# Layer 0's softmax sums over keys: folded from 128 to 64 partitions and summed for two steps in one TensorE pass, a group later

## The chip, the core and the metric

The kernel runs on one core of a Trainium2 chip. The time is the device time of one execution in microseconds (us); lower is better. In the profile PE is TensorE (PEld its weight loads), DVE is VectorE, ACT is ScalarE, POOL is GpSimd, and SP is SyncE, whose queue issues most of the DMAs. A name like L443 is line 443 of the kernel before.

## The reference

Two cross attentions follow each other. Layer 0 takes x (2 x 2048 x 512) as queries and a context of 128 tokens per batch as keys and values, with 16 heads of 64 and a mask over the keys:

```python
attn = jnp.einsum('bqhd,bkhd->hbqk', qh, kh)
attn = attn * mask[None]
attn = attn - jnp.max(attn)
attn = jnp.exp(attn) * mask[None]
attn = attn / (jnp.sum(attn, axis=-1, keepdims=True) + 1e-15)
out = jnp.einsum('hbqk,bkhd->bqhd', attn, vh).reshape(Bn, Tq, H * DK)
out = out @ Wo + bo
x = out + residual          # and a layer norm with gamma and beta
```

Layer 1 is a plain softmax attention of 16 heads of 32 on the result, again with residual and layer norm. The change concerns one term of layer 0: `jnp.sum(attn, axis=-1)`, the sum over the 128 keys for each query and head. All is in 32-bit floats.

## The kernel before, in words

The queries are cut into NB = 8 blocks t of TB = 512 tokens, and layer 0's heads into NG = 4 groups g of four heads. A pair (t, g) is one step; the list `order` holds the 32 steps so that two steps of the same g and neighbouring blocks stand together. The loop at the end of layer 0 (its variable is i, from 0 to 15) takes two steps at a time; one turn of it is called a group below. The order of the instructions on every engine is the order in which the program is written, since the schedule is manual; tiles wait for each other through buffers that rotate in their pool (two `mm` and two `av` buffers in PSUM, four `p1` buffers of which each holds the probabilities of one step).

A turn of the loop with i > 0 does this:

- `queries_pair` makes the queries of the two steps with seven half-size products (L347, TensorE) in the order 1, 6, 7, 2, 5, 4, 3. Each product is two matmuls into one PSUM buffer. ScalarE copies product 1 (L368) and VectorE adds the others up (L359, L361). Between these, `exponentials0` is called for the two steps of the previous group, `before[0]` after product 1 and `before[1]` after product 2's addition: VectorE reduces the maxima of all partitions (L428, L429), ScalarE takes the exponentials (L432), and GpSimd multiplies with the mask (L433). So the reduction for `before[1]` stands in VectorE's queue ahead of the two additions that read product 5.
- `scores0` of the first step: TensorE multiplies keys and queries (L395, `st`), the keys on the 128 partitions of the result. VectorE applies the mask and takes each partition's maximum (L407). SyncE writes the maxima to DRAM (L416, `top`), waits for this to land, and reads them back onto all partitions (L419, `every`).
- `attend0` of the first step of the previous group: four matmuls with a matrix of ones (L443, `den`), one for each head and side by side in four column strips of 32, sum the probabilities over the keys; ScalarE copies the sums out (L445). Eight matmuls (L451, `psu`) multiply the probabilities with the values in two halves, and ScalarE copies each (L455). SyncE stores the sums (L456, 8 KB) and the result (L459, `u`, 512 KB).
- `scores0` and `attend0` again, for the second step of the group and the second of the group before.

SyncE's queue thus holds per group: `top`, `every`, `den`, `u`, and once more `top`, `every`, `den`, `u`. In some groups loads of x and masks (the masks on GpSimd's queue) come first, and `token_sums_1` and `token_sums_2` put eight additions on VectorE when g is 3. While p is 0 (i from 0 to 3) `keys0` comes ahead of the queries. In the last turn only the first `attend0` is called; the last three steps are attended to after the loop, and then layer 1 begins. Layer 1's own order is written out in `steps`. The rows g1 and b1, layer 1's gamma and beta, are loaded during layer 0's start and first used in layer 1.

Of the kernel before, what the change touches and what calls it, by code (L numbers as in the profile page):

```python
# [16 lines left out]
P = 128  # L17
# [7 lines left out]
def two_cross_attentions(  # L25
# [98 lines left out]
    def chunks(w):  # L124
        return w.rearrange("(c p) m -> p c m", p=P)
# [80 lines left out]
    with tc.tile_pool(name="w1", bufs=1) as w1, tc.tile_pool(name="a2", bufs=2) as a2, tc.tile_pool(  # L206
# [129 lines left out]
        def queries_pair(p, g, before):  # L336

            a, b = 2 * p, 2 * p + 1
            e0, e1 = 2 * g, 2 * g + 1
            (a11, a12), (a21, a22) = halves0(g)  # L340
            (b11, b21), (b12, b22) = xts[a], xts[b]
            t1, t2, t4 = zip(*(token_sums[p, c] for c in range(2)))

            def product(n, w, x, tile_of):
                ps = tile_of(f"ps{n}_{p}_{g}")
                for c in range(2):
                    nc.tensor.matmul(  # L347
                        ps, w[:, c, :], x[c] if isinstance(x, tuple) else x[:, c, :],
                        start=(c == 0), stop=(c == 1),
                    )  # L350
                return ps

            def q_tile(t, e):
                queries[t, e] = four.tile([P, TB], F32, tag="q", name=f"q0_{t}_{e}")
                return queries[t, e]

            def add(out, ps, sb, bias=None):
                if bias is None:
                    nc.vector.tensor_tensor(out, ps, sb, ALU.add)  # L359
                else:  # L360
                    nc.vector.scalar_tensor_tensor(  # L361
                        out=out, in0=ps, scalar=bias, in1=sb, op0=ALU.add, op1=ALU.add
                    )

            less1 = db0[:, e0 : e0 + 1]
            c11 = q_tile(a, e0)
            ps = product(1, a11, b11, mm_tile)
            nc.scalar.activation(c11, ps, AF.Identity, bias=bq0s[:, e1 : e1 + 1])  # L368
            exponentials0(*before[0])
            c12 = q_tile(b, e0)  # L370
            add(c12, product(6, s2[:, g], t2, mm_tile), c11)
            c21 = q_tile(a, e1)
            add(c21, product(7, a21, b12, av_tile), c12)
            add(c11, product(2, a12, b21, av_tile), c11, less1)
            exponentials0(*before[1])
            c22 = q_tile(b, e1)
            ps = product(5, s1[:, g], t1, mm_tile)
            add(c22, ps, c21)
            add(c12, ps, c12, less1)
            add(c21, product(4, a22, t4, mm_tile), c21)  # L380
            add(c12, product(3, s4[:, g], b22, av_tile), c12)

        tops0, probs0 = {}, {}
        last4 = w1.tile([P, 4], F32, tag="last4", name="last4")
        order = [(2 * p + n, g) for p in range(NB // 2) for g in range(NG) for n in range(2)]

        def scores0(t, g):

            b, _ = where(t)
            st = sc_tiles(f"st_{t}_{g}", [2, TB])  # L390
            for n in range(2):
                q = queries.pop((t, 2 * g + n))
                for j in range(2):
                    rows = slice(j * DK, (j + 1) * DK)
                    nc.tensor.matmul(  # L395
                        st[n][:, j, :], k0[rows, 2 * g + n, b * K : (b + 1) * K], q[rows, :],
                        start=True, stop=True,
                    )
            pair = fours.tile([P, 2, 2, TB], F32, tag="p1", name=f"sm_{t}_{g}")
            n0 = 2 * (order.index((t, g)) - len(order) + 2)  # L400
            if n0 >= 0:
                top = last4[:, n0 : n0 + 2]
            else:
                top = a2.tile([P, 2], F32, tag="top", name=f"top_{t}_{g}")
            for n in range(2):
                sm = pair[:, n]
                nc.vector.tensor_tensor_reduce(  # L407
                    out=sm, in0=st[n], in1=masks[t].unsqueeze(1).to_broadcast([P, 2, TB]),
                    scale=1.0, scalar=-3.4028234e38, op0=ALU.mult, op1=ALU.max,
                    accum_out=top[:, n : n + 1],  # L410
                )
                probs0[t, 2 * g + n] = sm
            if n0 >= 0:
                return

            nc.sync.dma_start(top_dram[t, g], top)  # L416
            every = a2.tile([P, 2 * P], F32, tag="every", name=f"every_{t}_{g}")
            flat = top_dram[t, g].rearrange("p n -> (p n)").unsqueeze(0)
            nc.sync.dma_start(every, flat.to_broadcast([P, 2 * P]))  # L419
            tops0[t, g] = every  # L420

        def exponentials0(t, g):
# [7 lines left out]
            for n in range(2):  # L430
# [3 lines left out]
                    s, s, masks[t].unsqueeze(1).to_broadcast([P, 2, TB]), ALU.mult  # L434
                )

        def attend0(t, g):

            b, _ = where(t)
            p = [probs0[t, 2 * g + j // 2][:, j % 2, :] for j in range(4)]  # L440
            ps = av_tile(f"den0_{t}_{g}")
            for j in range(4):
                nc.tensor.matmul(ps[32 * j : 32 * (j + 1), :], ones, p[j], start=True, stop=True)  # L443
            den = a4.tile([P, TB], F32, tag="den", name=f"dens0_{t}_{g}")
            nc.scalar.copy(den, ps)  # L445
            u = a3.tile([P, 2, TB], F32, tag="u", name=f"u0_{t}_{g}")
            for half in range(2):
                ps = av_tile(f"psu0_{t}_{g}_{half}")
                for j in range(4):
                    d = (4 * g + j) * DK + half * 32  # L450
                    nc.tensor.matmul(  # L451
                        ps[32 * j : 32 * (j + 1), :], v0[:, b, d : d + 32], p[j],
                        start=True, stop=True,
                    )
                nc.scalar.copy(u[:, half, :], ps)  # L455
            nc.sync.dma_start(  # L456
                den_rows(den_dram, t, g), den.rearrange("(j n) q -> j n q", n=32)[:, 0, :]
            )
            nc.sync.dma_start(u_dram[t, g], u.rearrange("p j q -> p (j q)"))  # L459

        bo0s, g0s = row(const, bo0, "bo0"), row(const, g0, "g0")
        g1s, b1s = row(const, g1, "g1"), row(const, b1, "b1")
        b0cs = columns(const, b0c, "b0c")
        g0cs = columns(const, g0c, "g0c")

# [10 lines left out]
        for i in range(len(order) // 2):  # L476
            p, g = i // NG, i % NG
            steps0 = order[2 * i : 2 * i + 2]
            if g == (2 if p == 0 else 1) and p + 1 < NB // 2:
                for t in (2 * p + 2, 2 * p + 3):  # L480
                    load_x(t)
                    masks[t] = load_mask(t)
            if p == 0:
                for e in (2 * g, 2 * g + 1):
                    keys0(e)
            if i == 1:
                for n in range(E // TB):
                    values0(1, n)
            if i == 4:
                w = w1.tile([P, 2 * ND, TB], F32, tag="first", name="wkv1")  # L490
                wk1s, wv1s = w[:, :ND, :], w[:, ND:, :]
                nc.sync.dma_start(wk1s, chunks(wk1))
                nc.sync.dma_start(wv1s, chunks(wv1))
            if i == 12:
                sums0(0, w1, "sums0", 1)
            if i == 13:
                load_wo0()

            if i == 0:
                queries0(0, 0)  # L500
                queries0(0, 1)
            else:
                queries_pair(p, g, order[2 * i - 2 : 2 * i])
            if i == len(order) // 2 - 1:
                for n in range(NG):
                    fetch_u(0, n)
            scores0(*steps0[0])
            if i == 0:
                queries0(1, 0)
                queries0(1, 1)  # L510
                weight_sums(1)
            else:
                attend0(*order[2 * i - 2])
            if i == 0:
                token_sums_1(0)
            elif g == NG - 1 and p + 1 < NB // 2:
                token_sums_1(p + 1)
            scores0(*steps0[1])
            if i == 0:
                for n in range(E // TB):  # L520
                    values0(0, n)
                token_sums_2(0)
                weight_sums(2)
            elif i < len(order) // 2 - 1:
                attend0(*order[2 * i - 1])
            if g == NG - 1 and p + 1 < NB // 2:
                token_sums_2(p + 1)
            if i in (1, 2):
                weight_sums((3, 0)[i - 1])
# [568 lines left out]
    for t in range(-1, NB):  # L1098
        go(steps(t))
        if t == -1:  # L1100
            nc.sync.dma_start(wo1s, chunks(wo1))
    t = NB - 1
    for i in range(NQ):
        project1(t, i, 0)
# [76 lines left out]
```

## Time and profile before

| what | value |
|---|---|
| median of 3 runs | 991.02 us (990.36 to 991.05) |
| the profiled execution | 989.38 us, of which the span of the core is 987.40 us |
| granted TensorE clock | 0.997 of full speed |
| TensorE busy, 45 to 398 us (layer 0's loop and its tail) | 353.0 of 353.0 us |
| VectorE, ScalarE, GpSimd busy in the same stretch | 184.5, 139.7, 158.5 us |
| one `den` matmul on record (L443), 256 records for 128 matmuls | 605 ns each, four at a time |
| ACT 128x2048 (L926); DVE 128x2048 (L858); POOL 128x1024 (L433) | 1912; 2278; 2368 ns |

A row of a timeline gives the start and duration in us, the engine, the line, the operation with its output and input, how many instructions were merged in the row, and in brackets how long the engine sat idle before it and what ended that. A matmul of 32-bit floats is on record twice, so "x8" are four matmuls. The chain of waits is followed back from the last instruction to what released each piece; a piece of it names what the end of the kernel depended on at that time.

### The profile page before, as it was taken

How to read it: one execution, taken by the hardware profiler on the slowest of the kernel's cores; microseconds unless marked ns; L12 is line 12 of the kernel's file. 1: busy time of each engine (PE TensorE's matmuls, PEld its weight loads, DVE VectorE, ACT ScalarE, POOL GpSimd, SP SyncE). 2: the span in 40 equal slices, each digit the busy share in tenths (PEclk: the TensorE clock that was granted, in tenths of full speed). 3: DMA queues.
4: the chain of work that ended last, by engine and by line, in shares of the span. 5: the costliest groups of instructions: out<-in, count | busy, mean ns of one | idle time of the engine just before them, and what ended most of it. 6: DMA issues, size and time to landing. Idle time of an engine off the chain costs nothing.

```text
span 987.4 us, 12723 instructions
## 1 busy us (share of the span) xinstructions
PE 968.7 (98%) x4628; PEld 451.3 (46%) x4628; DVE 658.9 (67%) x1060; ACT 382.4 (39%) x626; POOL 483.4 (49%) x403
## 2 busy tenths in 40 slices
PE   9999999999999999999999999999999999999996
PEld 5444333333333334474634644645545545445432
DVE  2544645565464553148569869869789689698866
ACT  1133434343443434134544434444344444344251
POOL 1043454443344455594454834925826736545143
PEclk9999999999999999999999999999999999999998
DMA  9324254124223443634643542632723724504311
GB/s 341 138 49 140 55 173 154 55 76 146 75 55 84 142 129 126 202 114 152 220 158 95 180 162 89 220 124 87 257 86 115 252 93 151 164 2 139 120 43 42
DMA packets 51325, 128.46 MB, mean 130 GB/s; under 512 B 9440, under 2 KB 13280, under 8 KB 47680
## 3 DMA queue, kind: packets, MB, share of 16 engines
q1 hardware_dynamic: 49536, 125.03, 38.4%
q0 software_dynamic: 1152, 2.10, 0.7%
q8 instruction: 36, 0.59, 0.3%
q10 hardware_dynamic: 576, 0.53, 0.2%
q14 instruction: 25, 0.20, 0.1%
HBM read 101.46 MB, written 26.18 MB: 129 GB/s over the span
## 4 chain that ended last, share of the span: by engine, by line
PE 88%; DVE 5%; DMA 3%; POOL 2%; issue 1%; ACT 1%; POOLq 0%; SPq 0%; DVEq 0%; ACTq 0%
PE pso L626 21%; PE ps L347 18%; PE pso L980 9%; PE psq L777 7%; PE st L395 6%; PE psu L451 5%; PE mx L828 3%; PE den L443 3%; PE s L902 3%; PE u L950 3%; DMA p<-rows 2%; PE psk L261 2%; PE psq L815 1%; PE psq L328 1%; PE psv L273 1%
## 5 line engine op out<-in xcount | busy, mean ns | idle before, releaser
L433 POOL TENSOR_TENSOR sm<-sm,mask 128x1024 f32<-128x1024 f32 x64 | 150.1, 2368 | 212.7 <-ACT sm L432 212.7
L626 PE MATMUL pso<-wo,uT 128*128 128x512 f32 x512 | 229.3, 599 | 0.5 <-POOL uT L182 0.5
L626 PEld LDWEIGHTS pso<-wo,uT 128*128 128x128 f32 x512 | 94.6, 190 | 117.5 <-issue 108.5
L613 POOL TENSOR_TENSOR rstd<-rstd,mhalf 128x1 f32<-128x1 f32 x64 | 35.2, 550 | 216.3 <-DVE shift L617 216.2
L980 PE MATMUL pso<-wq,ctx 128*128 128x512 f32 x256 | 115.4, 600 | 0.0
L407 DVE CUSTOM_DVE_ANT_1 sm<-st,mask 128x1024 f32<-128x1024 f32 x64 | 75.8, 1221 | 47.9 <-issue 23.5
L432 ACT ACTIVATE sm<-sm,ncs 128x1024 f32<-128x1024 f32 x64 | 69.9, 1140 | 70.1 <-DVE ncs L429 69.9
L844 ACT ACTIVATE e<-mx,less 128x128 f32<-128x128 f32 x224 | 61.0, 383 | 83.3 <-DVE less L841 83.3
L921 DVE TENSOR_TENSOR p<-s,p 128x1024 f32<-128x1024 f32 x56 | 65.9, 1219 | 40.2 <-PE s L902 28.1
L926 ACT ACTIVATE p<-p 128x2048 f32<-128x2048 f32 x28 | 53.5, 1912 | 97.0 <-DVE p L921 95.5
L359 DVE TENSOR_TENSOR q<-ps,q 128x512 f32<-128x512 f32 x75 | 51.6, 689 | 59.1 <-PE ps L347 31.8
L347 PE MATMUL ps<-xt,wq 128*128 128x512 f32 x180 | 83.4, 599 | 0.0
L182 POOL TENSOR_TENSOR uT<-uT,r 128x1024 f32<-128x1024 f32 x32 | 75.3, 2363 | 6.3 <-issue 3.8
L980 PEld LDWEIGHTS pso<-wq,ctx 128*128 128x128 f32 x256 | 46.6, 190 | 58.0 <-issue 51.0
L858 DVE TENSOR_REDUCE sums<-e 128x16 f32<-128x2048 f32 x28 | 63.8, 2278 | 1.1 <-ACT e L852 1.1
L395 PE MATMUL st<-q,k 64*128 64x512 f32 x256 | 63.6, 615 | 0.0
L451 PE MATMUL psu<-sm,v 128*32 128x512 f32 x512 | 62.6, 598 | 0.0
L347 PE MATMUL ps<-t,s 128*128 128x512 f32 x120 | 56.4, 592 | 0.0
L347 PEld LDWEIGHTS ps<-xt,wq 128*128 128x128 f32 x180 | 33.2, 190 | 46.5 <-issue 43.8
L445 ACT COPY dens<-den 128x512 f32<-128x512 f32 x32 | 18.8, 588 | 89.8 <-PE den L443 89.8
L641 ACT ACTIVATE z<-z,shift,rstd 128x512 f32<-128x512 f32 x32 | 26.1, 815 | 67.3 <-POOL shift L618 67.3
L643 POOL TENSOR_TENSOR y<-z,g 128x512 f32<-128x512 f32 x32 | 40.7, 1270 | 23.2 <-ACT z L641 23.2
(149 smaller groups left out, 1466.0 us busy)
## 6 DMA issues: line engine op xcount, KB each, us to landing
p<-rows SPq DMA_DIRECT2D x28, 1024.0 KB
u<-u SPq DMA_DIRECT2D x32, 512.0 KB
uT<-u SPq DMA_DIRECT2D x32, 512.0 KB
xt<-in_xT_dram SPq DMA_DIRECT2D x16, 512.0 KB
z<-in_x_dram SPq DMA_DIRECT2D x32, 256.0 KB
r<-r SPq DMA_DIRECT2D x32, 256.0 KB
out_dram<-y SPq DMA_DIRECT2D x32, 256.0 KB
r<-rows SPq DMA_DIRECT2D x28, 256.0 KB
```

The costliest lines, as they stand in the source:

```text
L182: nc.gpsimd.tensor_tensor(u, u, r.unsqueeze(1).to_broadcast([P, 2, TB]), ALU.mult)
L347: nc.tensor.matmul(ps, w[:, c, :], x[c] if isinstance(x, tuple) else x[:, c, :], start=(c == 0), stop=(c == 1),)
L395: nc.tensor.matmul(st[n][:, j, :], k0[rows, 2 * g + n, b * K : (b + 1) * K], q[rows, :], start=True, stop=True,)
L407: nc.vector.tensor_tensor_reduce(out=sm, in0=st[n], in1=masks[t].unsqueeze(1).to_broadcast([P, 2, TB]), scale=1.0, scalar=-3.4028234e38, o ...
L432: nc.scalar.activation(s, s, AF.Exp, bias=ncs[:, i + n : i + n + 1])
L433: nc.gpsimd.tensor_tensor(s, s, masks[t].unsqueeze(1).to_broadcast([P, 2, TB]), ALU.mult)
L451: nc.tensor.matmul(ps[32 * j : 32 * (j + 1), :], v0[:, b, d : d + 32], p[j], start=True, stop=True,)
L626: nc.tensor.matmul(ps, uTs[t, n // 2][:, n % 2, i * P : (i + 1) * P], wo0s[n // 2][:, n % 2, :], start=(n == 0), stop=(n == NE - 1),)
L777: nc.tensor.matmul(ps[:, m, :], w[:, c, m * P : (m + 1) * P], y[:, c, :], start=(c == 0), stop=(c == 1),)
L858: nc.vector.tensor_reduce(to.rearrange("p r i o -> p r (i o)"), open_x.pop((t, g)), AX.X, ALU.add)
L921: nc.vector.tensor_tensor(p1[:, at], ps[n], p1[:, at], ALU.subtract)
L980: nc.tensor.matmul(ps, ctxs[t][g][:, i * P : (i + 1) * P], wo1s[:, g, :], start=(g == 0), stop=(g == NG - 1),)
```

## The change

The sums are no longer made step by step on 128 keys, except for the last four steps. For a pair of steps i - 1 (there are 14 such pairs, FOLDED = 14) a tile `fold` is filled: ScalarE copies the upper 64 keys of the first step to partitions 0 to 63 (`shift(i - 1, 0)`), and the lower 64 keys of the second step to partitions 64 to 127 (`shift(i - 1, 1)`), each 64x2048. GpSimd adds the lower keys of the first step to its copy, VectorE the upper keys of the second to its own (`fold`). In the next turn of the loop, after the queries and ahead of the first scores, `sums_of_folded` sums the 64 partitions of both steps with eight matmuls of 64 rows and 32 columns into two `av` buffers, ScalarE copies these out and SyncE stores them. The `den` matmuls, copy and DMA of `attend0` go for these pairs. Product 3 of the queries takes an `mm` buffer in place of an `av` buffer, the `den` tile has two buffers in place of four, and the rows g1 and b1 are loaded after the first list of layer 1.

```diff
-            add(c12, product(3, s4[:, g], b22, av_tile), c12)
+            add(c12, product(3, s4[:, g], b22, mm_tile), c12)
...
+        FOLDED = NB // 2 * NG - 2
...
+        def store_sums(t, g, ps):
+            den = a2.tile([P, TB], F32, tag="den", name=f"dens0_{t}_{g}")
+            nc.scalar.copy(den, ps)
+            nc.sync.dma_start(
+                den_rows(den_dram, t, g), den.rearrange("(j n) q -> j n q", n=32)[:, 0, :]
+            )
...
+        def half_keys(n):
+            return slice(n * P // 2, (n + 1) * P // 2)
...
+        def shift(i, n):
+            if n == 0:
+                folded[i] = w1.tile([P, 4, TB], F32, tag="fold", name=f"fold_{i}")
+            p = pairs0[order[2 * i + n]].rearrange("p n j q -> p (n j) q")
+            nc.scalar.copy(folded[i][half_keys(n)], p[half_keys(1 - n)])
...
+        def fold(i, n):
+            p = pairs0[order[2 * i + n]].rearrange("p n j q -> p (n j) q")
+            f = folded[i][half_keys(n)]
+            (nc.vector if n else nc.gpsimd).tensor_tensor(f, f, p[half_keys(n)], ALU.add)
...
+        def sums_of_folded(i):
+            f = folded.pop(i)
+            ps = [av_tile(f"den0_{i}_{n}") for n in range(2)]
+            for j in range(4):
+                for n in range(2):
+                    rows = slice(n * P // 2, (n + 1) * P // 2)
+                    nc.tensor.matmul(
+                        ps[n][32 * j : 32 * (j + 1), :], ones[rows, :], f[rows, j, :],
+                        start=True, stop=True,
+                    )
+            for n in range(2):
+                store_sums(*order[2 * i + n], ps[n])
...
         def attend0(t, g):
...
-            ps = av_tile(f"den0_{t}_{g}")
-            for j in range(4):
-                nc.tensor.matmul(ps[32 * j : 32 * (j + 1), :], ones, p[j], start=True, stop=True)
-            den = a4.tile([P, TB], F32, tag="den", name=f"dens0_{t}_{g}")
-            nc.scalar.copy(den, ps)
+            if order.index((t, g)) // 2 >= FOLDED:
+                ps = av_tile(f"den0_{t}_{g}")
+                for j in range(4):
+                    nc.tensor.matmul(ps[32 * j : 32 * (j + 1), :], ones, p[j], start=True, stop=True)
+                store_sums(t, g, ps)
...
-            nc.sync.dma_start(
-                den_rows(den_dram, t, g), den.rearrange("(j n) q -> j n q", n=32)[:, 0, :]
-            )
...
                 queries_pair(p, g, order[2 * i - 2 : 2 * i])
+                if i > 1:
+                    sums_of_folded(i - 2)
...
             else:
+                if i - 1 < FOLDED:
+                    shift(i - 1, 0)
+                    fold(i - 1, 0)
                 attend0(*order[2 * i - 2])
+                if i - 1 < FOLDED:
+                    shift(i - 1, 1)
...
                 attend0(*order[2 * i - 1])
+                fold(i - 1, 1)
...
             nc.sync.dma_start(wo1s, chunks(wo1))
+            g1s, b1s = row(one, g1, "g1"), row(one, b1, "b1")
```

## The prediction, made before the result was known

> **What bounds the kernel now.** I read the page's busy row first.
>
> ```profile
> PE 968.7 (98%) x4628; PEld 451.3 (46%) x4628; DVE 658.9 (67%) x1060; ACT 382.4 (39%) x626; POOL 483.4 (49%) x403
> ```
>
> TensorE is busy 98% of the span, so a pass of TensorE taken away is time, unless a wait takes its place. Next, the chain of waits over one group of layer 0 (two steps of `order`):
>
> ```profile
> 225.20 12.21 PE ps L347 x28
> 237.42 1.92 PE st L395 x8
> 239.33 1.00 PE den L443 x8
> 240.33 1.77 PE psu L451 x16
> ...
> 246.79 12.21 PE ps L347 x28
> ```
>
> A group takes 246.79 - 225.20 = 21.59 us, with no gap. To see how near the other engines are, I read TensorE's, VectorE's and SyncE's timelines from these scores to the next group's end. TensorE (start, duration):
>
> ```profile
> 242.03 1.99 PE L395 MATMUL st<-q,k 64*128 64x512 f32 x8
> 243.95 1.06 PE L443 MATMUL den<-sm,ones 128*32 128x512 f32 x8
> 244.83 1.96 PE L451 MATMUL psu<-sm,v 128*32 128x512 f32 x16
> ...
> 255.41 1.88 PE L347 MATMUL ps<-t,wq 128*128 128x512 f32 x4
> 257.13 1.88 PE L347 MATMUL ps<-xt,s 128*128 128x512 f32 x4
> ```
>
> The last two are products 4 and 3; product 5 ends as product 4 begins. VectorE beside them:
>
> ```profile
> 255.38 0.42 DVE L428 TENSOR_REDUCE whole<-every 128x2 f32<-128x256 f32 x1 [0.74 <-DMA every<-top]
> 255.84 0.17 DVE L429 TENSOR_SCALAR ncs<-whole 128x2 f32<-128x2 f32 x1
> 255.91 0.68 DVE L359 TENSOR_TENSOR q<-ps,q 128x512 f32<-128x512 f32 x1
> 256.51 0.74 DVE L361 SCALAR_TENSOR_TENSOR q<-ps,db,q 128x512 f32<-128x512 f32 x1
> ```
>
> The two additions that read product 5 are queued behind the reduction of the second step's maxima, which waits for a DMA. They end at 257.25, 1.84 after product 5. Today nobody waits for that. Product 4 began at 255.41, so it isn't in product 5's buffer: the two `mm` buffers alternate. SyncE's queue shows why the maxima are late:
>
> ```profile
> 241.02 0.33 SPq L416 DMA_DIRECT2D top<-top  x1
> 243.86 0.33 SPq L419 DMA_DIRECT2D every<-top  x1
> 244.28 0.50 SPq L456 DMA_DIRECT2D den<-dens  x1
> 244.87 0.39 SPq L459 DMA_DIRECT2D u<-u  x1
> 245.71 1.38 SPq L416 DMA_DIRECT2D top<-top  x1
> 251.71 0.32 SPq L419 DMA_DIRECT2D every<-top  x1
> ```
>
> The second `top` goes out behind the 512 KB of `u`; its landing, which line 419 waits for, comes 6.84 us after `u` was issued.
>
> **What the change removes and adds on TensorE.** It removes two of the `den` passes of a group. In the timeline one takes 244.83 - 243.95 = 0.88 us from start to start (the chain's 1.00 holds the switch from the 64*128 scores to 128*32, which stays, since `psu` follows in the same form). It adds one pass of eight 64*32 tiles. No row has that form; its bounds are one pass (0.88, as eight tiles at once) and two (1.77). Line 395 runs 64-row tiles two at once, line 443 32-column tiles four at once, so I take one, plus 0.09 for a switch. The rule against this is the Trainium skill, TensorEngine Tiling (Array Packing), section Key Properties: a change of tiling mode drains TensorE. The change brings a mode between 128*128 and 64*128 and takes no switch away. The trace prices a switch at about 0.1 (1.00 - 0.88); one gives 0.97 a pass, two would give 1.1 and 2 us more in all. Saved per group: 2 x 0.885 - 0.97 = 0.80; over 14 folded pairs 11.2 us, if nothing waits.
>
> **The wait that it adds.** Product 3 moves from an `av` to an `mm` buffer. The alternation gives it product 5's, so it must wait for both additions of product 5. Behind it on TensorE stand the sums, the scores and the whole next group; VectorE's maxima, and with them SyncE, wait for the scores. When do these additions end after the change? I count from the first scores S of a group (237.35 above), with the mean of the 12 groups in which the maxima's DMA came last (those whose queries start from 117.27 on; before them `keys0` adds 3.5 us of cover):
> - first `top` issued: S + 3.67 (VectorE's two maxima passes, as now);
> - landed and `every` issued: 3.18 (2.76 to 4.30, the longest beside mask loads);
> - `u` issued: 0.42, as the `den` DMA between them (0.59) is gone; its copies end by S + 4.5, see below;
> - second `every` issued: 7.07 (6.37 to 7.77);
> - reduction starts: 3.38 (2.92 to 4.27).
> So the reduction starts at S + 17.72; at present 18.35 by the same rows. The additions end 1.88 later (255.38 to 257.25), and a weight load released by VectorE costs TensorE some 0.15 (an estimate from two restarts of the timeline in layer 1, where VectorE ended at 475.23 and 478.01 and the waiting weight loads began at 475.29 and 478.07, and from the 0.1 by which a block after a gap is longer, 1.98 against 1.88). Product 3 can start at S + 19.75. Unhindered it would start at 257.13 - 237.35 - 1.77 = S + 18.01. The stall is 1.74 us a group, since what saves time on TensorE doesn't move the maxima's DMA: the period is 19.75 + 1.81 (product 3) + 0.97 = 22.53 against 21.59. Twelve groups lose 0.94 each, 11.3 us; the two groups before them gain 0.80 each. Sum: +9.7 us.
>
> **What lies beside other work.** ScalarE: 28 copies 64x2048. The nearest row, 128x2048 at line 926, is 1.91; bounds 1.91 and 3.8 if half the lanes cost double, and I take 1.91, as a copy's time goes by elements per partition (0.36 for 256, 0.59 for 512). After the sums come two `den` copies (S + 0.15 to 1.3), the first shift to 3.3, the `u` copies to 4.5, the second shift to 6.4. `u` is issued at S + 7.3, so 2.8 are spare; a shift over 4.7 us would begin to cost. The second shift needs the mask products of the second step: 2.2 for the exponentials and 4.7 for GpSimd after the reduction end by the next S + 2. GpSimd: 14 additions 64x2048; 1.27 for 512 and 2.37 for 1024 give 4.6. It runs S + 3.3 to 7.9; behind it wait the mask loads and the next mask product, due at S + 11.4. VectorE: 14 at 2.28 (128x2048 at line 858), queued ahead of the first reduction: S + 7.4 to 9.7; that reduction starts at S + 10.4 now. The Trainium skill, GPSIMD Engine Reference, section Specifications, says that GpSimd contends with VectorE's instructions with two SBUF inputs, which this one is. The trace has no such pair side by side (the maxima at 1.22, beside GpSimd or not, have one). At GpSimd's 4.6 us the addition ends at S + 12, and the first addition of queries slips by 1.5; product 4, its next user, comes at S + 16. Both give zero. In the three groups after token sums the delay reaches product 7, about 1 us, but inside the later wait of product 3. The longer-held `sm` buffers are free (S + 9.7) before they are written again; one `fold` tile is free as soon as the sums have read it, ahead of the next shift. The `den` DMAs now precede the first `top` in SyncE's queue: issued by S + 2, `top` at S + 3.67. The uT fetches of the last group slip behind them by some 6 us; their user on GpSimd starts at 393, 26 us later. The rows g1, b1 (two issues of 0.5, 512 KB) move from the start to behind wo1's load at 441.92, ahead of `z` and `r` loads first used some 40 us later: zero, at most 1 to 2 us without that cover. Their absence from the start could gain at most the 2 us that TensorE idles in the first 45; I take none.
>
> **Sum.** The profiled execution took 989.38 (span 987.40); +9.7 gives 999.1. It lies 1.6 under the median of 991.02, so the forecast on that is 1000.7.
>
> **Rivals.** (1) The wait is hidden and the passes are simply saved: 991.0 - 11.2 = 979.8, faster. For it: ScalarE, GpSimd and VectorE are all idle half of this stage. Against it: even today the reduction starts 7.6 to 9.9 us into a group, and product 3 tolerates 8.4. It decides at a reduction at S + 16.0; between that and 17.72, break-even is S + 16.9 (0.93 stall a group). The earliest single group would be at 17.0. Chance 0.13, and 0.07 that shorter DMA times end within 0.2%. (2) The 64*32 tiles take two passes, or another queue (shift, fold) holds more: +0.885 x 14 = 12.4 on the forecast, 1013. For it: no row has the form. Chance 0.10. (3) The forecast, 995 to 1007, as 0.4 us more or less in the DMA chain is 5 us over twelve groups: 0.70. Within 0.2% (about 2 us, what can be told from no change): 0.07; slower 0.80. The range 989 to 1011 leaves out (1) and most of (2).
>
> **What would show it.** In the profile after: product 3's weight loads in `ps<-xt,s` idle about 1.7 us on VectorE in twelve groups; the period 22.5; the new `den` pass near 0.97; the second reduction some 17.7 after the scores; VectorE's wait for `every` longer than now. If the period is 20.8 with no idle TensorE, rival 1 holds; a `den` pass near 1.9 shows rival 2. The forecast is wrong if `u` or `top` land faster by over 0.8 us.

## The result and the profile after

| kernel | median | runs | against before |
|---|---|---|---|
| before, beside it | 991.03 us | 990.36 to 991.34 | 1 |
| after | 1035.67 us | 1034.56 to 1041.0 | 1.046, 95% interval 1.043 to 1.049 |

The change costs 44.6 us; 9.7 were forecast. The profiled execution of after, the slowest of the four, took 1041.0 us (span 1038.9), 51.5 us of span more than before. Its busy row, and the row of granted clocks in 40 slices:

```profile
PE 980.5 (94%) x4628; PEld 453.0 (44%) x4628; DVE 708.7 (68%) x1074; ACT 433.7 (42%) x654; POOL 546.6 (53%) x417
...
PEclk9999898999998999999999999999999999999998
```

TensorE does as many matmuls as before (4628 records), but falls from 98% busy to 94% of a longer span, and is nevertheless busy 11.8 us longer: it both waits and runs slower. All but 2 of the 51.5 us lie between the first scores of the loop's second turn and those of its sixteenth: 309.1 us before, 358.8 after. The fourteen periods in it were 25.0 twice and 21.6 twelve times; after they are 24.8, 24.2, 28.7, 27.4, 24.8, 23.6, 28.3, 26.1, 24.9, 22.7, 28.3, 26.4, 24.9 and 23.7. (The forecast's were 24.2 and then 22.5.)

The chain of waits over the group that the forecast followed (start, duration, what):

```profile
247.20 7.91 DMA top<-top
255.13 4.27 DMA every<-top
...
259.42 0.43 DVE whole L430
...
260.04 0.59 DVE q L359
260.63 0.67 DVE q L361
...
261.35 3.00 PE ps L347 x4
264.34 1.63 PE den L470 x16
```

Before, this chain was TensorE alone. Now it runs through the second maxima's two DMA trips (the first starts behind `u`, issued at 246.77), VectorE's reduction, both additions of product 5, and only then product 3 (261.35), as forecast. TensorE's timeline shows the size, and a second effect:

```profile
208.53 1.98 PE L347 MATMUL ps<-xt,s 128*128 128x512 f32 x4 [2.51 <-DVE q L361]
...
261.35 3.00 PE L347 MATMUL ps<-xt,s 128*128 128x512 f32 x4 [3.48 <-DVE q L361]
264.27 1.70 PE L470 MATMUL den<-fold,ones 64*32 64x512 f32 x16
...
286.34 3.53 PE L347 MATMUL ps<-xt,s 128*128 128x512 f32 x4 [2.33 <-DVE q L361]
```

Product 3 (the second row) waits 3.48, and then its two matmuls take 3.00 us in place of 1.88 to 1.98, and the pass of sums 1.70 in place of 1.09. The clock is the reason, as windows of the profile show it. A row gives the window and its length; the busy time of TensorE, its weight loads, VectorE, ScalarE and GpSimd, with their instructions; then the granted clock, the DMA share and GB/s. Here are the groups whose first scores were at 107.0 and 187.9:

```profile
107.00:135.70 28.70, 24.35 (x100) 8.47 (x92) 22.05 (x28) 12.17 (x13) 13.85 (x6) 0.88 0.38 120
...
187.90:211.40 23.50, 20.99 (x100) 7.55 (x92) 13.19 (x20) 12.18 (x13) 12.23 (x6) 1.00 0.20 57
```

The same hundred records take 24.35 us at a clock of 0.88 and 20.99 at 1.00. In before the clock was 1.00 from 117 to 376 us. In after the granted clock, between 100 and 400 us, was always either 1.00 or 0.50, and all its 18 changes lie whole numbers of 3.413 us apart. So time falls into slots of 3.41 us. Cut at these points, the profile shows the waits of 2.51 us (which ended at 208.53) and of 2.33 (286.34) so:

```profile
204.15:207.56 3.41, 1.87 (x5) 0.57 (x3) 0.92 (x3) 0.24 (x1) 1.13 (x1) 1.00 0.52 192
207.56:210.97 3.41, 2.44 (x20) 0.86 (x20) 1.93 (x4) 1.95 (x2) 2.42 (x2) 1.00 0.02 5
...
282.66:286.07 3.41, 1.35 (x4) 0.29 (x2) 1.62 (x4) 0.94 (x1) 0.67 (x1) 1.00 0.49 185
286.07:289.48 3.41, 3.14 (x4) 1.17 (x4) 0.81 (x2) 1.25 (x2) 3.12 (x2) 0.50 0.00 0
289.48:292.89 3.41, 3.41 (x29) 1.02 (x32) 1.49 (x2) 1.84 (x3) 1.54 (x1) 1.00 0.01 2
```

The longer wait is split between two slots, which hold 1.54 and 0.97 us of idle TensorE, and nothing follows. The shorter one leaves 2.06 idle in one slot, and the next slot runs at 0.50.

The list of TensorE's waits in this stretch has two that cost (us in all, times, longest):

```profile
PE ps L347 <- DVE q L361: 25.3, 12, 3.7
PE ps L347 <- issue: 12.8, 3, 4.3
```

The first is the forecast's, at 25.3 for its 20.9. The second is product 7's in the three groups with token sums, which the forecast had as a delay of about 1 us inside the other wait. VectorE, GpSimd and TensorE there:

```profile
110.56 4.81 DVE L309 TENSOR_TENSOR t<-xt,xt 128x512 f32<-128x512 f32 x1
115.41 0.69 DVE L310 TENSOR_TENSOR t<-xt,t 128x512 f32<-128x512 f32 x1
...
119.75 2.29 DVE L462 TENSOR_TENSOR fold<-fold,sm 64x2048 f32<-64x2048 f32 x1
122.06 0.69 DVE L318 TENSOR_TENSOR xt<-xt,xt 128x512 f32<-128x512 f32 x1
```

```profile
110.28 4.54 POOL L462 TENSOR_TENSOR fold<-fold,sm 64x2048 f32<-64x2048 f32 x1 [1.98 <-ACT fold L456]
```

```profile
122.86 6.75 PE L347 MATMUL ps<-xt,wq 128*128 128x512 f32 x8 [4.25 <-issue]
```

A token-sum subtraction that takes 0.69 us (the second row) took 4.81: it began 0.28 after GpSimd's fold addition, and ended at 115.37, 0.55 after that one's end (110.28 + 4.54 = 114.82). Everything behind it on VectorE slips by 4.1, and by 2.3 more behind VectorE's own fold (L462), down to `token_sums_2` (L318), which writes the `xt` that product 7 reads. It ends at 122.75, and product 7 starts at 122.86: the profile names no releaser here, but the program and these times do. TensorE idles 4.25 us, and then takes 6.75 for products 7 and 2 in place of 3.60.

Before, the same two rows had room between them (first scores at 107.82):

```profile
116.33 0.69 DVE L318 TENSOR_TENSOR xt<-xt,xt 128x512 f32<-128x512 f32 x1
120.73 3.60 PE L347 MATMUL ps<-xt,wq 128*128 128x512 f32 x8
```

L318 ended 9.2 us after the first scores, and product 7 came at 12.9. In after product 6 begins at 116.37, and where nothing waits product 7 begins 1.72 us behind it: that would be 118.09, 11.1 after the scores, since the two passes of sums no longer stand between. With 0.1 for TensorE to start, product 7's slack was 3.6 us; the change itself takes 1.8 of that away.

The passes themselves came out as forecast: the eight 64*32 tiles go in one pass, 1.02 us to the next start where 0.97 was forecast, and 1.77 for two passes.

### The profile page after: what moved, and what is told of

Its sections match the earlier page's. It is cut to its first block, busy times and chain, and to the rows that moved or that the text cites. A ratio compares the mean times of both kernels' runs of the same rounds, so it can differ in the third digit from the quotient of the medians.

```text
span 1038.9 us, 12762 instructions
## 1 busy us (share of the span) xinstructions
PE 980.5 (94%) x4628; PEld 453.0 (44%) x4628; DVE 708.7 (68%) x1074; ACT 433.7 (42%) x654; POOL 546.6 (53%) x417
## 4 chain that ended last, share of the span: by engine, by line
PE 67%; DMA 16%; DVE 10%; issue 3%; POOL 2%; ACT 1%; SPq 0%; POOLq 0%; DVEq 0%; ACTq 0%
PE pso L670 19%; PE pso L1024 9%; DMA top<-top 8%; PE ps L347 8%; PE psq L821 6%; PE st L396 4%; DMA every<-top 4%; PE mx L872 3%; PE s L946 3%; PE psu L491 2%; PE u L994 2%; DMA p<-rows 2%; PE den L470 2%; DVE sm L409 2%; DVE t L309 2%
## 5 line engine op out<-in xcount | busy, mean ns | idle before, releaser
L409 DVE CUSTOM_DVE_ANT_1 sm<-st,mask 128x1024 f32<-128x1024 f32 x64 | 75.8, 1221 | 54.1 <-PE st L396 40.2
L347 PE MATMUL ps<-xt,wq 128*128 128x512 f32 x180 | 90.7, 643 | 12.8 <-issue 12.8
L462 POOL TENSOR_TENSOR fold<-fold,sm 64x2048 f32<-64x2048 f32 x14 | 63.8, 4560 | 31.5 <-ACT fold L456 31.5
L347 PEld LDWEIGHTS ps<-xt,wq 128*128 128x128 f32 x180 | 35.3, 204 | 64.6 <-issue 62.3
L347 PE MATMUL ps<-xt,s 128*128 128x512 f32 x60 | 37.9, 766 | 25.3 <-DVE q L361 25.3
L685 ACT ACTIVATE z<-z,shift,rstd 128x512 f32<-128x512 f32 x32 | 26.1, 814 | 68.6 <-POOL shift L662 68.6
```

Source lines behind the costliest of these rows:

```text
L347: nc.tensor.matmul(ps, w[:, c, :], x[c] if isinstance(x, tuple) else x[:, c, :], start=(c == 0), stop=(c == 1),)
L409: nc.vector.tensor_tensor_reduce(out=sm, in0=st[n], in1=masks[t].unsqueeze(1).to_broadcast([P, 2, TB]), scale=1.0, scalar=-3.4028234e38, o ...
L462: (nc.vector if n else nc.gpsimd).tensor_tensor(f, f, p[half_keys(n)], ALU.add)
```

## The experiments

Theory A: the time is lost in product 3's wait behind the reduction (one word of the diff makes it), in GpSimd's addition holding up VectorE's token sums, and in the clock that drops after such waits. Theory B, the rival: the added copies and additions, or the new pass, hold something else. All ratios are to the kernel before, run on the same chip beside them.

### The wait of product 3

**e1_mm_alone** is before with only this word:

```diff
-            add(c12, product(3, s4[:, g], b22, av_tile), c12)
+            add(c12, product(3, s4[:, g], b22, mm_tile), c12)
```

> The kernel before with one part of the change alone: product 3 takes the mm buffer of product 5. Theory (product 3 waits for the two additions that VectorE holds behind the maxima's DMA): in the 12 groups from the fourth on the reduction starts 7.6 to 9.9 us into a group where 8.38 is tolerated; the excesses add up to 6.5 us, so about 997.5, with product 3 waiting for VectorE in some ten groups, longest 1.5. Rival (the loss comes from the folding work itself, and the buffer costs nothing): 991.

Measured: 1007.35 us, 1.0166 (1.0151 to 1.0181). Nothing is folded, and the one word costs 16 us. Product 3 waits for VectorE's `q` 11 times, 11.8 us in all; once like this, with the scores behind it:

```profile
151.67 2.73 PE L347 MATMUL ps<-xt,s 128*128 128x512 f32 x4 [1.92 <-DVE q L361]
154.33 2.88 PE L395 MATMUL st<-q,k 64*128 64x512 f32 x8
```

The mechanism is shown, and it cost more than the 6.5 us expected: the waits alone were 11.8, and one slot of half clock cost 1.7 more (product 3 took 2.73 here and the scores 2.88 in place of 1.99). After another wait of 2.37 both were at full speed (1.98 and 1.99).

**e2_reduce_later** is after with the second step's reduction moved behind both additions of product 5, so that these no longer stand behind its DMA:

```diff
             add(c11, product(2, a12, b21, av_tile), c11, less1)
-            exponentials0(*before[1])
...
             add(c12, ps, c12, less1)
+            exponentials0(*before[1])
             add(c21, product(4, a22, t4, mm_tile), c21)
```

> The changed kernel with the second step's reduction, exponentials and mask products moved behind the two additions that read product 5, so that these no longer stand behind the maxima's DMA. Theory: product 3 no longer waits (25 us of idle TensorE gone) and the slow clock after these waits is gone (some 10 us); what stays is the three groups after token sums, with 4.25 us each of waiting before product 7 and slow matmuls after it, some 20 us: about 1000. Rival (the folding work holds the chain, not the order on VectorE): 1030 or more.

Measured: 1007.23 us, 1.0166 (1.0149 to 1.0183): 28.4 of the 44.6 us come back from an order of instructions alone. TensorE's waits:

```profile
PE ps L347 <- issue: 12.8, 3, 4.3
...
PE ps L347 <- DVE q L361: 0.7, 1, 0.7
```

Product 3's wait is 0.7 us (the two rows left out, 2.4 and 2.3 us, are other matmuls' waits). Of the twelve periods from the third on five are 20.8 to 20.9, the forecast's unhindered one; three are 27.3, 30.6 and 28.4, those with token sums. They are 23.9 us over 20.8, in place of the 20 that were expected. So theory A stands, and most of the rest is theirs.

### GpSimd beside the token sums

**e3_three_not_folded** is after with the three pairs not folded whose fold addition falls beside token sums (`folds(i)` stands in place of `i < FOLDED`; these three sum as before):

```diff
+        def folds(i):
+            return 0 <= i < FOLDED and i not in (2, 6, 10)
```

> The changed kernel without folding in the three pairs whose folding lies in a group with token sums (pairs 2, 6 and 10 keep the den matmuls). Theory (GpSimd's addition stretches VectorE's first token sum from 0.69 to 4.8 us, and product 7 then waits): the token sum is back at 0.69, product 7 doesn't wait; but product 3 waits in the next group as it does elsewhere, so these groups go from 28.4 to about 25.5: 1035.7 - 9 = 1027. Rival (VectorE's queue is just too long there, GpSimd doesn't matter): the token sum stays at 4.8 in no trace, but product 7 still waits some 3 us, and the time is 1035 to 1038.

Measured: 1027.73 us, 1.0377 (1.0357 to 1.0398). The subtraction at L309 is back at 0.69, product 7's wait is gone, and the three periods fall from 28.3 - 28.7 to 22.1 - 22.5. But only 8 us come of it, since the groups behind them now wait fully for product 3 (12 waits, 29.1 us in all). The edit takes all of the folding out of these groups, VectorE's addition with GpSimd's.

**e4_both** has e2's and e3's edits.

> Both of these edits together: no folding in the three groups with token sums, and the second reduction behind product 5's additions. Theory: no waits of TensorE in layer 0's loop, the clock at 1.00, eleven folded pairs that save 0.8 each: 991 - 9 = 982, faster than both kernels. Rival (a third cause, such as the shifts on ScalarE or the pass of eight tiles): above 991.

Measured: 987.06 us, 0.9962 (0.9947 to 0.9977), 0.4% faster than before, though 5 us short of what was expected. Both costs are thus named: they are worth 48.6 us together. GpSimd's hold on VectorE shows here on the fold itself:

```profile
244.16 4.38 DVE L465 TENSOR_TENSOR fold<-fold,sm 64x2048 f32<-64x2048 f32 x1
```

```profile
241.82 4.56 POOL L465 TENSOR_TENSOR fold<-fold,sm 64x2048 f32<-64x2048 f32 x1
```

Alone this addition takes 2.29 (L462 above). It began 2.22 before GpSimd's ended (246.38), and ended at 248.54, 2.16 after it: it made next to no progress meanwhile.

**e6_gpsimd_alone** adds to before nothing but a GpSimd addition of that size in each group but the last, on a spare tile that nobody reads (g1, b1 and the `den` buffers as in after, so that it fits):

```diff
             else:
+                if i < 15:
+                    nc.gpsimd.tensor_tensor(spare[:64], spare[:64], spare[:64], ALU.add)
                 attend0(*order[2 * i - 2])
```

> The kernel before, with one GpSimd addition of 64x2048 on a spare tile per group, where the change puts its fold, and nothing else of the change on the engines (the rows g1, b1 and the den buffers move as in the change, to make room). Theory (GpSimd's two-input addition holds up VectorE's additions of two SBUF inputs): the first token sum, 0.69 before, is stretched to the end of GpSimd's addition, 3.5 to 4.5 us, in the three groups that have it, and product 7 then waits 1 to 2 us there: 994 to 1000. Rival (VectorE's first token sum waits in the changed kernel for its own queue or data): 0.69 and 991.

Measured: 993.78 us, 1.0028 (1.0016 to 1.004). VectorE and GpSimd beside the first token sums:

```profile
110.66 1.22 DVE L409 CUSTOM_DVE_ANT_1 sm<-st,mask 128x1024 f32<-128x1024 f32 x1
...
111.80 2.87 DVE L309 TENSOR_TENSOR t<-xt,xt 128x512 f32<-128x512 f32 x1
```

```profile
110.53 3.59 POOL L515 TENSOR_TENSOR spare<-spare 64x2048 f32<-64x2048 f32 x1
```

With no dependence between them, the subtraction ended 0.55 after GpSimd's end (114.12), again; the maxima pass of L409 ran beside GpSimd at its usual 1.22. It reads one operand from PSUM; both of L309's are in SBUF. So the hold is GpSimd's, without the rest of the change. The cost that was expected of it, 1 to 2 us of waiting for product 7 in each of the three groups, did not come. In the third group GpSimd's mask products and this addition held VectorE for 4.2 us in all, as long as in after, and product 7 waited 0.29:

```profile
286.66 1.56 DVE L309 TENSOR_TENSOR t<-xt,xt 128x512 f32<-128x512 f32 x1
288.26 3.97 DVE L310 TENSOR_TENSOR t<-xt,t 128x512 f32<-128x512 f32 x1
```

```profile
296.55 4.00 PE L347 MATMUL ps<-xt,wq 128*128 128x512 f32 x8 [0.29 <-issue]
```

Here product 7 still has the slack of 3.6 us, and no fold stands ahead of `token_sums_2`. In after the slack is 1.8. By that sum the hold of 4.1 alone would make product 7 wait 2.3 us, and VectorE's fold of 2.3 makes it 4.6; the trace has an idle time of 4.25 behind a product 6 that is 0.36 longer on record. No run has one without the other in after's order, so this split is worked out, not tried.

### The clock

**e5_filled** is after with one product issued twice from the second pair of blocks on (product 4, or 6 when g is 0), so that TensorE works into its waits (the second time overwrites the first).

```diff
-                for c in range(2):
+                again = 2 if p and n == (6 if g == 0 else 4) else 1
+                for k in range(2 * again):
+                    c = k % 2
```

> The changed kernel with TensorE kept at work in the waits: in the twelve groups of p > 0 product 4 is computed twice into the same buffer (product 6 in the groups with g = 0), 1.75 us of matmuls more per group, 21 us in all, with the same result. The wait of product 3 still ends with VectorE's additions. Theory (the matmuls after a wait are slow because the clock drops when TensorE idles): the clock stays near 1.00, product 3 takes 1.9 to 2.0 everywhere, and the 11 us of slow products 3 and most of the 7 us of slow products 7 are gone: 1018, faster with more work. Rival (they are slow for another reason, or the waits grow with the work): 1035 to 1050.

Measured: 1034.26 us, 1.0442 (1.0418 to 1.0465), the time of after, where 1018 was expected. In the profiled execution product 3 waits 11.9 us and product 7 7.6, in place of 25.3 and 12.8, so 18.6 us of waiting have gone. The time at half clock fell from 41.0 to 13.7 us; TensorE was busy for 13.6 of these 13.7, so its matmuls lost half of that, 6.8 us, in place of 18.3 in after. Against this stand twelve products of 1.72, 20.6 us. The sum, 20.6 - 18.6 - 11.5, is -9.5, and the span is 8.9 shorter (1030.0 against 1038.9); by the medians the gain is only 1.4. So shorter waits do bring the clock back, and the work that fills them costs about what it brings.

### The DMA chain of the second maxima

**e7_u_later** is after with the first step's `u` stored behind the second step's `every`, to test whether its 512 KB ahead of `top` make the maxima late.

```diff
-                attend0(*order[2 * i - 2])
+                store_u = attend0(*order[2 * i - 2], later=True)
...
             scores0(*steps0[1])
+            if i > 0:
+                store_u()
```

> The changed kernel with the first step's u stored behind the second step's maxima on SyncE's queue (the order of the DMAs alone is changed). Theory (the maxima are late because they queue behind 512 KB of u): the second reduction starts some 14 us after the first scores in place of 18.5 to 19.8, product 3 doesn't wait, and only the three groups after token sums are left: 1000 to 1007, as when the reduction is moved. Rival (the maxima are late because of the engines that make them): 1025 or more.

Measured: 1013.25 us, 1.0224 (1.0205 to 1.0242), where 1000 to 1007 was expected: 22 us back, but product 3 still waits 9.3 us in 11 groups. Without `u` ahead, the maxima still need three trips in series: `top` 3 us, the second `top` behind the first `every` 5.3, the second `every` 4.5, so that the reduction comes at about S + 17.3. That `u` alone makes them late is thus wrong; it is part. The Trainium skill, DMA: Bandwidth & Descriptors, section Queues, rings and completion order, says that a DMA's completion lands only after all earlier writes of the same DMA engine: so a small store reports late behind a large one. The runs agree as far as they go: `top` lands 3 us after its issue with no store ahead of it, and 7.9 behind `u` (the chain of after).

**e8_u_later_three_not_folded** adds e3's edit.

> As the run before, and without folding in the three pairs beside token sums. Theory: no wait of TensorE is left in layer 0's loop; eleven folded pairs save 0.8 each: 982; at least as fast as the version that moves the reduction (987.1), whose exponentials come late for the second step. Rival: a further cost of the folding shows, 987 or more.

Measured: 993.68 us, 1.0033 (1.0019 to 1.0048), where 982 was expected, a miss for the same reason: product 3 waits 9.3 us in 9 groups.

**e10_reduce_and_u_later** has all three edits.

> The version with the reduction behind product 2's addition and three groups not folded (987.06 us), and in it the first step's u stored behind the second step's every, so that the second maxima arrive about 1 us a group sooner. If what is left there (TensorE waiting for ScalarE's den copies, 3.8 us in 5 groups, and for the next exponentials) comes from the lateness of the second maxima, those waits vanish: 982 to 985 us. The rival, that what is left comes from the longer queue on ScalarE itself, gives 986 to 989, and u stored later could cost in the u tile's buffers.

("Behind product 2's addition" there is e2's edit, which puts it behind product 5's.)

Measured: 981.59 us (981.45 to 982.03) beside 992.01, 0.9897 (0.988 to 0.9914), the best of all and at the fast end of what was expected. The chain of waits is TensorE alone again, with a period of 20.77:

```profile
219.52 12.21 PE ps L347 x28
231.73 1.02 PE den L473 x16
...
240.29 12.21 PE ps L347 x28
```

**e11 to e15** ask why `u` to the second `every`, 7.1 us before, takes longer once pairs are folded. Four are e4 with work left out, and their lines below are against e4: e11 leaves out GpSimd's additions, e12 VectorE's, e13 the shifts, e14 all three (the sums of folded steps then lack keys; TensorE and SyncE's queue are unchanged). e15 is before with `u` stored ahead of `den`. The first lines are e11's, the second e12's, the rest e13's:

```diff
                     shift(i - 1, 0)
-                    fold(i - 1, 0)
...
-                if folds(i - 1):
-                    fold(i - 1, 1)
...
+        spare = w1.tile([P, 4, TB], F32, tag="fold", name="spare")
+        nc.vector.memset(spare, 0.0)
...
-            nc.scalar.copy(folded[i][half_keys(n)], p[half_keys(1 - n)])
+                folded[i] = spare
```

And e15:

```diff
+            nc.sync.dma_start(u_dram[t, g], u.rearrange("p j q -> p (j q)"))
             nc.sync.dma_start(
                 den_rows(den_dram, t, g), den.rearrange("(j n) q -> j n q", n=32)[:, 0, :]
             )
-            nc.sync.dma_start(u_dram[t, g], u.rearrange("p j q -> p (j q)"))
```

> The same version without GpSimd's fold additions (the lower keys of each folded first step are left out of its sum). Question: why does the time from the issue of u to the issue of the second every grow from 7.1 us to about 9.0 in folded groups? If GpSimd's addition slows the DMA or its issue, it falls to about 7 to 7.6 us here; if VectorE's addition or ScalarE's shift does, it stays near 9. The time itself: within 3 us of 987.

> The same version without VectorE's fold additions (the upper keys of each folded second step are left out of its sum). If VectorE's addition is what holds back the path from u to the second every (it stands ahead of the maxima reduction on VectorE), the time from u to the second every falls to about 7 to 7.6 us; if GpSimd's does, it stays near 9. Time 984 to 988.

> The same version without ScalarE's shifts (the fold tile is zeroed once, so that the moved half of the keys is missing and the sums run on). If the shift, which stands ahead of the u copies, is what delays u, top and the second every, then the time from u to the second every falls and the TensorE waits for ScalarE vanish: 982 to 985 us. If the additions do it, it stays near 9 and the time near 987.

> The 987 us version without shifts and without both fold additions (the fold tile is zero, so the sums of the folded steps are zero); TensorE's passes and SyncE's queue are as in it. If the engines' work together causes the 9.1 us from u to the second every in folded groups, it falls to 7.0 to 7.5. If the queue's order does, it stays at 8.3 or above. Time 980 to 986 either way.

> The kernel before with the two stores of a step in the other order, u ahead of den; all else is as it was. If u's place directly behind every on the queue lengthens its way, the time from u to the second every rises from 7.07 to 8.3 us or more (the den store between them counts for up to 0.6 of that); if the engines' work is the cause, it stays at 7.1 to 7.6. Nobody waits for it in this kernel: 990 to 993 us.

Measured, in one execution each for e11 to e15; the last two columns are means by SyncE's timeline, over the eleven groups folded in e4, and for before, e15 and after over the twelve groups of the forecast:

| kernel | time | `u` to second `every` | first to second `every` |
|---|---|---|---|
| before | 991.0 | 7.07 | 8.11 |
| e15, `u` ahead of `den` | 991.5 | 7.96 | 8.37 |
| after | 1035.7 | 8.29 | 8.71 |
| e4 | 987.1 | 9.11 | 9.53 |
| e11, no GpSimd | 986.9 | 8.36 | 8.78 |
| e12, no VectorE | 988.9 | 9.06 | 9.48 |
| e13, no shifts | 987.2 | 8.74 | 9.16 |
| e14, no work | 986.6 | 8.46 | 8.88 |

SyncE's queue in e15:

```profile
244.27 0.33 SPq L419 DMA_DIRECT2D every<-top  x1
244.68 0.38 SPq L456 DMA_DIRECT2D u<-u  x1
...
252.62 0.32 SPq L419 DMA_DIRECT2D every<-top  x1
```

With no other work added, sending `u` 0.6 us earlier, straight behind `every`, brings the second `every` no earlier (8.37 after the first, against 8.11). That is 0.88 of the 1.22 us by which the forecast's 7.49 was short. From `u` on it is 7.96, between the two answers that were set down for it (8.3 and more, 7.1 to 7.6), so the queue's order explains most of the growth and not all. In e4 the engines' work adds about 0.65 (9.53 against 8.88), GpSimd's the most by these means, but single groups scatter by 1 us and more, so which engine it is stays open. Without the shifts (e13) TensorE still waits 3.5 us for ScalarE's copies of the sums, so the gain expected there did not come. The times of e11 to e14, single as they are, also say that the added work on ScalarE, VectorE and GpSimd costs e4 next to nothing, which leaves nothing to theory B beyond GpSimd's hold on VectorE; what held e4 back was `u` on the queue, which e10 moves.

## Why the prediction was wrong

The sign and the wait of product 3 were right, the size wrong by 35 us. Two costs were put at nothing, product 7's wait (12.8 us) and the slow clock behind both waits (18.1), and product 3's wait was put 4.4 too low. In the profiled execution the fourteen periods would be 2 x 24.2 + 12 x 20.8 = 298.0 unhindered, and were 358.8.

- **The saving** was right: 309.1 - 298.0 = 11.1 against 11.2, with the pass at its forecast length; rival 2 falls. e2, e4 and e10 show the period of 20.8.
- **Product 3's wait** was right in kind, and mis-sized: 25.3 us against 20.9. The term was the DMA chain, from the first `every` to the second: 0.42 + 7.07 = 7.49 forecast, 8.71 measured. The step took 0.6 off because the `den` store leaves the queue; e15 shows that `u`, sent earlier, doesn't land its successors earlier. The sum of 25.3 hides part of the error: in the three groups with token sums product 3 hardly waits (at most 0.6), as the wait of product 7 has covered it, and in the other nine it waits 2.69 us each in place of 1.74.
- **"In the three groups after token sums the delay reaches product 7, about 1 us, but inside the later wait of product 3"** is the step that failed most clearly. It put at nothing what came to 12.8 us. It asked only for the fold's own delay. The rule on two SBUF inputs was applied to one VectorE instruction, the fold, and not to the token sums' subtractions, which have two SBUF inputs too and start beside GpSimd's addition in exactly these groups. The Trainium skill, SBUF — State Buffer, section Who interferes with whom, calls the shared ports an exclusive lock; by that rule, applied to these rows, the subtraction would have been held for up to GpSimd's 4.6 us, and the trace has 4.81 for its 0.69. Nor did the forecast see that product 7 comes 1.8 us sooner after the scores once the passes of sums have gone. The wait is 4.25 three times, 12.8 us, and covers product 3's, not the reverse. e3 and e4 show that the folding in these groups makes it, e6 that GpSimd alone holds VectorE; the shares of GpSimd's and VectorE's additions are worked out.
- **The clock** had no term: product 3 was taken at 1.81 and the sums at 0.97 after a stall. The slow records are product 3's (six of them 2.89 to 3.78 in place of 1.98, 8.5 us), the sums behind (2.3) and products 7 and 2 (5.45 to 6.75 in place of 3.60, 7.3): 18.1 us. The clock accounts for them: it was at 0.50 nine times, for one slot or two, 41.0 us in all. TensorE was busy for 36.6 us of these, and half of that is 18.3. Between 100 and 400 us every matmul record that lies wholly in these stretches took 1.06 us or more (61 records), and every one wholly outside 0.70 or less (986). The Trainium skill, TensorE: Matmul & The Clock Gate, Part 1, says that TensorE's clock drops to half after an idle window of about 3.4 us that runs freely. The trace agrees on half and on windows of 3.41 us on a grid of their own, but not that a window must be idle throughout: the nine slots ahead of the drops held 1.96 to 3.41 us of idle TensorE, and no slot at full clock that held 1.66 or less was followed by one. In other runs 1.72 was once enough (e12) and 1.98 once not (e1). So a wait's length alone doesn't decide it; how much of it falls into one slot does, and the slots lie differently in each trace (counted from the span's start, whole slots and 2.76 us in after, 2.58 in e1, 2.13 in e5).

Together 25.3 + 12.8 + 18.1 = 56.2 of the 60.8 us over 298.0; 4.6 I can't assign. Rival 1 (979.8) is nearly what e10 comes to, at 981.6, by the order of two steps and with three pairs left unfolded: the passes are worth what was said, once nothing waits.

## What to carry to other kernels

Before passes are taken off a busy engine, ask for each buffer whose readers stand in an in-order queue behind a DMA's wait: freed passes don't move that DMA, and a tile moved to such a buffer (one word) can cost more than they save. Price a stall of TensorE with the matmuls behind it at half clock, once some 2 us of stalls can fall into one slot of 3.4 us, as here. Price the queue's trips in series as they are measured, without taking off a small store that leaves. When work goes to GpSimd, list every VectorE instruction with two SBUF inputs that can fall beside it, not only the new ones, and take the slack behind them from the new order: passes that leave TensorE bring the next reader sooner.

## What the runs showed of the hardware

- A VectorE addition or subtraction with both inputs in SBUF hardly moved while GpSimd's addition ran: 0.69 became 4.81, 2.87 and 3.97, 2.29 became 4.38, each ending no more than its own duration after GpSimd's end. Passes with an input in PSUM kept their time (1.22).
- Eight matmuls of 64 rows and 32 columns run in one pass: 1.02 us to the next start.
- TensorE's granted clock changed only at points whole numbers of 3.41 us apart. In after it fell to half behind the nine slots in which TensorE was idle for 1.96 us or more, for one slot or two; waits of 2.13 to 2.33 us brought that when all or nearly all of them lay in one slot, and one of 2.51 that was split between two did not.
- On one queue, a 512 KB store sent 0.6 us earlier behind a 128 KB load didn't bring the small store behind it, and the load that waits for it, any earlier (8.11 to 8.37 us from load to load).
